# Attention preparation: head products copied to SBUF by ScalarE before the multiplications, column sums with the rows as moving operand, and the first transposes placed ahead of the weight preparation

## The chip, the cores and the metric

The kernel runs on one core of a Trainium2 chip. The metric is the device time of one execution in microseconds (us), taken as the median of several runs. Engines are named as in the profile: PE is TensorE, with PEld for its weight loads; DVE is VectorE; ACT is ScalarE; POOL is GpSimd; SP is SyncE, which here only issues DMAs.

## What is computed

The reference is a two-layer network over 4096 nodes with 256 features. Each layer is a graph attention followed by a feed-forward part, both with a residual. There are three attentions in all (one in layer 0, two in a row in layer 1), and the change touches the preparation of these three:

```python
def attention(x, adj, W, a1, a2):                 # 4 heads of 64
    h = einsum('nf,hfd->hnd', x, W)               # products
    f1, f2 = einsum('hnd,hd->hn', h, a1), einsum('hnd,hd->hn', h, a2)
    e = leaky_relu(f1[:, :, None] + f2[:, None, :], 0.2)
    e = where(adj > 0, e, -9e15)
    return elu(einsum('hnm,hmd->hnd', softmax(e), h))

x = x + attention(layernorm(x), adj, L0)          # g0
x = x + ffn30(layernorm(x))                       # 30 steps of tanh, silu, layernorm, matmul
x = x + attention(attention(layernorm(x), adj, L1a), adj, L1b)   # g1, g2
x = x + mixture_of_experts(layernorm(x))          # 6 experts, top 2
```

## The kernel before

All tiles have 128 partitions. The 4096 nodes are 32 tiles, worked in 8 groups (`NG`) of 4 tiles (`G`). One function, `attention`, is called three times, under the names g0, g1 and g2. It has two stages: a preparation, which this change edits, and a long main stage, which it leaves alone. The main stage cannot begin before the preparation's buffers are given back.

The preparation runs a loop over `g`. For each group it does the following.

- `load(g)` (L260) fetches the group's 512 rows, 512 KB, through SP's queue, two groups ahead. In g0 these land in the tile `t`, which has three buffers; in g1 and g2 in `rows`.
- `columns(g)` (L270) transposes the rows on PE (L114) and copies them out of PSUM on ACT as `xT` (L278, or L281 in g2, which collects the column sums `xs` as it copies). Where the input is normalised (`norm`, in g0 and g1), `over_std` computes 1/std: `bn_stats` and `bn_aggr` on DVE (L101, L103) and a power on POOL (L106).
- `products(g)` (L299) multiplies with the weights on PE (L307). Its results lie in two PSUM tiles, `ph0` and `ph1`, of two node tiles each, with 256 head products and 8 logit columns for each node tile. The pool has one buffer for each, so the next group's products can only be written when all readers of this group's are done. DVE takes the logits out as `fs` (L320 or L324) and forms `gm` (L328). ACT makes the exponentials `bd` (L331), POOL multiplies them with signs (L332) and with 1/std to `b` (L362). PE transposes the logits (L336) into a small PSUM tile `sp` with one buffer. In g0 and g1, PE also computes the sums of the rows weighted by 1/std (L344): the 128x128 blocks of rows are the weights loaded into the array, and 1/std is the moving operand, one column. ACT copies them to `xs` (L351) and the logits to `rt` (L353), which SP stores to `fd`.
- `upper(g)` (L367) multiplies the products, read from PSUM, with `b` into two tiles `v` (DVE, L377, four instructions of 128x512), and ACT writes their fp16 upper halves to `vals` (L384). POOL fills one column of each `v` (L373).
- `lower(g)` (L386) writes the fp16 lower halves on DVE (L389, two instructions of 128x1040).

In g0 the loop also turns the adjacency of the first four row tiles into masks: POOL issues the loads (L209), PE transposes (L219), DVE compares (L227, L229). After the loop the sums of `xs` are spread by POOL (L442) and multiplied with the weights on PE (L445), and ACT scales the result into `hs` (L446).

`weights(...)` gives for each attention a pair: `load`, whose DMAs ACT issues, and `make`, which computes the logit columns of the weights on DVE (L159, L160) and, with `norm`, subtracts their means (L166 on PE, L168 on DVE). The preparation of g0 carries out all three `make`: g0's own ahead of the loop, the others at `g` 3 and 5.

The order of the calls inside one round of the loop is: load(g+2), columns(g), products(g-1), lower(g-2), upper(g-1), masks. For the first two groups `columns(g)` comes after `lower(g-2)`. The order in which each engine's queue finally holds the instructions is set by the framework's planner from this program order and its own estimate of when each instruction can run. Only in the main stage is the order of DVE and ACT fixed by hand.

## Time and profile before

| | |
|---|---|
| median of 3 runs | 3557.42 us (3556.58 to 3568.16) |
| profiled execution, its own time | 3558.91 us |
| its span, first to last instruction | 3557.2 us |
| mean granted TensorE clock | 0.967 |
| preparation of g0, by the trace | from the start to 124.7 us |
| preparation of g1 | 1900 to 1988.9 us |
| preparation of g2 | 2566.5 to 2625.8 us |

The profiled execution lies 1.5 us above the median, so a difference worked out in its trace may be taken from either. The three preparations hold about 273 us of the span. The page's shares of busy time are means over stages with quite different limits, so the preparations are read by themselves: busy time by stretch, who waited for whom in a stretch, and the instructions in order of time. In the profile a matmul of two fp32 operands shows as two instructions, so `x16` on L307 is eight matmuls. In the view of instructions in order of time, a line gives start, duration, engine, line and operation, and in brackets the idle time of the engine before it with what ended it.

### The profile page before, as it was taken

The numbers are of one execution on the slowest core, as the hardware profiler recorded it, in microseconds if no ns is written. First come the engines' busy times: TensorE is split into PE (matmuls) and PEld (weight loads), VectorE is DVE, ScalarE is ACT, GpSimd is POOL, SyncE is SP. The second block draws the span as 40 slices with busy tenths as digits, with TensorE's granted clock in tenths as the row PEclk, the third lists the DMA queues.
The fourth block names the chain that finished last, engine by engine and source line by source line (L and its number), as shares of the span: only waits on it lengthen the run. The fifth ranks groups of instructions, "written<-read, shape, count | busy, mean of one in ns | idle before, by whom it ended". The sixth has DMA issues, their size and how long they took to land. (4 is left out here: it accounts for less than half of the span.)

```text
span 3557.2 us, 80784 instructions
## 1 busy us (share of the span) xinstructions
PE 3272.9 (92%) x33523; PEld 2963.8 (83%) x33523; DVE 3010.9 (85%) x6039; ACT 2613.4 (73%) x2902; POOL 1101.7 (31%) x899
## 2 busy tenths in 40 slices
PE   6889999996999999999998899999979999995995
PEld 5778888885888888888887799999869999993784
DVE  6899999997887877778787799999989999997445
ACT  2688888895766666666663799999879999992221
POOL 3210101004877777777772000000000000001662
PEclk8899999998999999999998899999999999997997
DMA  6796886602000000000006021313221331314224
GB/s 137 139 234 134 196 189 139 189 17 60 1 1 1 1 1 1 1 1 1 1 1 220 14 92 50 123 30 113 79 97 46 111 120 37 120 37 148 90 90 182
DMA packets 280200, 288.47 MB, mean 81 GB/s; under 512 B 97149, under 2 KB 230426, under 8 KB 279834
## 3 DMA queue, kind: packets, MB, share of 16 engines
q1 hardware_dynamic: 198770, 224.18, 19.2%
q0 software_dynamic: 73920, 52.97, 9.7%
q10 hardware_dynamic: 7144, 6.16, 0.6%
q8 instruction: 264, 4.33, 0.5%
q14 instruction: 102, 0.84, 0.1%
HBM read 248.01 MB, written 68.81 MB: 89 GB/s over the span
## 5 line engine op out<-in xcount | busy, mean ns | idle before, releaser
L556 PE MATMUL acc<-vals,m 128*128 128x130 f16 (+1 forms) x19456 | 1723.4, 233 | 83.0 <-DVE m L619 42.7
L470 ACT ACTIVATE st<-f1b,f2b 128x1024 bf16<-128x1024 f32 (+2 forms) x1664 | 1659.4, 1073 | 100.1 <-DVE m L604 92.1
L556 PEld LDWEIGHTS <-m 128*128 128x128 bf16 x19456 | 1518.3, 98 | 181.3 <-DVE m L619 64.9
L604 DVE TENSOR_TENSOR m<-st,m 128x2048 bf16<-128x2048 bf16 (+2 forms) x832 | 929.0, 1134 | 12.4 <-ACT st L470 12.3
L774 PE MATMUL po<-wT,zT 128*128 128x256 f32 x3840 | 874.1, 381 | 13.3 <-ACT zT L800 12.3
L774 PEld LDWEIGHTS po<-wT,zT 128*128 128x128 f32 x3840 | 713.6, 191 | 104.2 <-ACT zT L800 14.8
L556 PE MATMUL acc<-vals,rows 128*128 128x130 f16 x5120 | 614.1, 221 | 15.1 <-DVE rows L619 15.1
L760 POOL TENSOR_TENSOR th<-th,y 128x1024 f32<-128x1024 f32 x240 | 567.5, 2366 | 192.8 <-ACT th L759 192.2
L106 POOL TENSOR_TENSOR ln_rstd<-ln_rstd,mhalf 128x4 f32<-128x4 f32 x272 | 282.4, 1039 | 881.6 <-DVE ln_rstd L105 676.4
L556 PEld LDWEIGHTS <-rows 128*128 128x128 bf16 x5120 | 490.0, 96 | 20.5 <-DVE rows L619 20.1
L101 DVE BATCH_NORM_STATS2 ln_st<-z 128x6 f32<-128x256 f32 x960 | 338.0, 414 | 190.5 <-ACT z L765 190.5
L800 ACT COPY zT<-tp 128x1024 f32<-128x1024 f32 x240 | 242.7, 1011 | 323.8 <-PE tp L114 323.8
L619 DVE TENSOR_TENSOR rows<-m,m 128x2048 bf16<-128x2048 bf16 x320 | 391.7, 1224 | 10.2
L784 DVE SCALAR_TENSOR_TENSOR y<-po,ln_rstd,bias 128x256 f32<-128x256 f32 x928 | 378.8, 470 | 6.6 <-PE po L774 5.9
L765 ACT ACTIVATE z<-th 128x1024 f32<-128x1024 f32 x240 | 254.5, 1060 | 17.4 <-POOL th L760 17.4
L114 PE MATMUL tp<-ident,z 128*128 128x128 f32 x1920 | 250.8, 274 | 8.8 <-ACT z L765 7.9
L114 PEld LDWEIGHTS tp<-ident,z 128*128 128x128 f32 x1920 | 225.3, 141 | 35.5 <-ACT z L765 10.5
L759 ACT ACTIVATE th<-y 128x1024 f32<-128x1024 f32 x240 | 251.3, 1048 | 4.8 <-DVE y L784 4.7
L209 POOL DMA_DIRECT2D rows<-in_adj_dram x80 | 72.9, 912 | 497.3 <-PE tp_m L219 488.2
L619 DVE TENSOR_TENSOR m<-m,m 128x1792 bf16<-128x1792 bf16 (+1 forms) x200 | 202.2, 1011 | 13.0 <-PE acc L556 0.5
L449 POOL MEMSET hs<- 128x4 f32 x3 | 0.3, 102 | 607.2 <-DVE u L500 585.9
L307 PE MATMUL ph<-g_w,xT 128*128 128x264 f32 x384 | 120.0, 477 | 30.9 <-DVE v L377 27.4
(212 smaller groups left out, 2319.7 us busy)
## 6 DMA issues: line engine op xcount, KB each, us to landing
m<-edges SPq DMA_DIRECT2D x32, 2048.0 KB, 9.9
rows<-in_adj_dram POOLq DMA_DIRECT2D x64, 448.0 KB
edges<-ms SPq DMA_DIRECT2D x64, 448.0 KB, 5.0
m<-edges SPq DMA_DIRECT2D x16, 1792.0 KB
f1b<-fd SPq DMA_DIRECT2D x32, 512.0 KB, 3.4
rows<-x1d SPq DMA_DIRECT2D x16, 512.0 KB, 6.3
y<-yd SPq DMA_DIRECT2D x16, 512.0 KB, 9.5
f1b<-fd SPq DMA_DIRECT2D x16, 448.0 KB, 3.3
```

Source lines behind the costliest of these rows:

```text
L101: nc.vector.bn_stats(st[:, r, :], src[:, r, :])
L106: nc.gpsimd.tensor_tensor(rstd, rstd, mhalf, OP.pow)
L114: nc.tensor.transpose(ps[:, k, r * P : (r + 1) * P], src[:, r, k * P : (k + 1) * P], ident)
L470: nc.scalar.activation(steps[at][:, s, :w], f1b[c, h][:, :w], AF.Relu, bias=f2b[:, 2 * q + s, h : h + 1], scale=BIG)
L556: nc.tensor.matmul(acc[:, i, cols], lhs[:, s, rows], v[:, cols], start=(j == 0 and n_ == 0), stop=(j == NT - 1 and n_ == 1), skip_group_ch ...
L604: nc.vector.tensor_tensor(m1[:, :, :w], st[:, :, :w], m, OP.logical_and if turned(q) else OP.min)
L619: nc.vector.tensor_tensor(m2[:, :, :w], m, m1[:, :, :w], OP.subtract)
L759: nc.scalar.activation(th[at], y[:, g * G : (g + 1) * G, :], AF.Tanh, scale=0.01)
L760: nc.gpsimd.tensor_tensor(th[at], th[at], y[:, g * G : (g + 1) * G, :], OP.add)
L765: nc.scalar.activation(z, th.pop(at - 1), AF.Silu, scale=0.01)
L774: nc.tensor.matmul(po[:, r, :], src[:, k, r * P : (r + 1) * P], wT[:, k, :], start=(k == 0), stop=(k == KC - 1),)
L784: nc.vector.scalar_tensor_tensor(y[:, g * G + r, :], po[:, r, :], rstd[:, r : r + 1], last if end else bias, op0=OP.mult, op1=OP.add,)
```

## The change

It has four edits, all in the preparation.

1. `products(g)` has a new SBUF tile `hc` (128x1024, fp32, one buffer). ACT copies the head products of `ph0` and `ph1` into it, right after the logits of each are taken. `upper` reads `hc` in place of the PSUM tiles, with one 128x1024 multiplication for each `v` in place of two of 128x512.
2. With `norm`, the weighted sums of the rows are formed with 1/std (one column) as the loaded weights and the rows (256 columns) as moving operand: four matmuls a group into one partition of `sp`, in place of eight with a moving operand of one column. DVE copies or adds them into `xs`, now one row of 256; the copies on ACT go.
3. After the loop, with `norm`, two matmuls with one row each turn `xs` into a column, which DVE copies, in place of a reduction.
4. g0's own `make` runs after `columns(0)`, inside the first round of the loop, and no longer ahead of the loop. Its DMAs are issued where they were.

```diff
-                xs = prep.tile([P, KC, NG], F32, name="xs")
+                xs = prep.tile([1, C] if norm else [P, KC, NG], F32, name="xs")
...
+                    hc = work.tile([P, G, C], F32, name="hc", bufs=1)
                     for i, ph in enumerate(phs):
...
+                        nc.scalar.copy(hc[:, 2 * i : 2 * i + 2, :], ph[:, :, :C])
...
-                        for k in range(KC):
-                            for i in range(G):
-                                nc.tensor.matmul(
-                                    pt[:, P + k : P + k + 1],
-                                    n[:, i, k * P : (k + 1) * P],
-                                    stds[g][:, i : i + 1],
-                                    start=(i == 0),
-                                    stop=(i == G - 1),
-                                )
-                        nc.scalar.copy(xs[:, :, g], pt[:, P : P + KC])
+                        for i in range(G):
+                            nc.tensor.matmul(
+                                pt[:1, P : P + C],
+                                stds[g][:, i : i + 1],
+                                n[:, i, :],
+                                start=(i == 0),
+                                stop=(i == G - 1),
+                            )
+                        if g == 0:
+                            nc.vector.tensor_copy(xs, pt[:1, P : P + C])
+                        else:
+                            nc.vector.tensor_tensor(xs, xs, pt[:1, P : P + C], OP.add)
...
-                    for i, ph in enumerate(phs):
-                        for part in range(2):
-                            nc.vector.tensor_tensor(
-                                vs[part][:, 2 * i : 2 * i + 2, :, :D],
-                                ph[:, :, :C].rearrange("p i (h o) -> p i h o", h=H),
-                                b[:, part, 2 * i : 2 * i + 2, :, None].to_broadcast([P, 2, H, D]),
-                                OP.mult,
-                            )
+                    for part in range(2):
+                        nc.vector.tensor_tensor(
+                            vs[part][:, :, :, :D],
+                            hc.rearrange("p i (h o) -> p i h o", h=H),
+                            b[:, part, :, :, None].to_broadcast([P, G, H, D]),
+                            OP.mult,
+                        )
...
-                if late:
-                    late.pop(0)()
...
                     if g < 2:
                         columns(g)
+                    if g == 0 and late:
+                        late.pop(0)()
...
-                nc.vector.tensor_reduce(xt, xs, axis=AX.X, op=OP.add)
+                if norm:
+                    pt = small_ps()
+                    for k in range(KC):
+                        nc.tensor.matmul(
+                            pt[:, k : k + 1], xs[:, k * P : (k + 1) * P], ones[:1, :1], start=True, stop=True
+                        )
+                    nc.vector.tensor_copy(xt, pt[:, :KC])
+                else:
+                    nc.vector.tensor_reduce(xt, xs, axis=AX.X, op=OP.add)
```

## The prediction, made before the change was run

> **What bounds the kernel now.** Of the three preparations I first read the busy time by stretch. One row each for g0, g1 and g2: start:end, length, then busy us of PE, PEld, DVE, ACT and POOL, the granted clock, the DMA share and GB/s.

> ```profile
> 22.00:124.70 102.70, 78.50 (x454) 64.84 (x454) 67.49 (x166) 29.70 (x57) 31.20 (x62) 0.79 0.63 122
> 1900.00:1987.40 87.40, 70.41 (x336) 57.15 (x335) 59.27 (x155) 32.27 (x59) 17.36 (x50) 0.80 0.48 165
> 2566.50:2625.80 59.30, 42.63 (x207) 33.91 (x207) 47.26 (x85) 32.43 (x75) 7.56 (x34) 0.96 0.60 206
> ```

> No engine is full: PE and DVE are busy 66 to 81% of the time, ACT 29 to 55%. So the groups are bound by waits on one another. Next, one group of g1 in order of time:

> ```profile
> 1962.92 2.48 DVE L377 TENSOR_TENSOR v<-ph,b 128x512 f32<-128x512 f32 x4 [1.45 <-POOL b L362]
> ...
> 1964.35 5.49 PE L307 MATMUL ph<-g_w,xT 128*128 128x264 f32 x16 [1.00 <-DVE v L377]
> ...
> 1969.88 0.17 DVE L320 TENSOR_TENSOR fs<-ph,ln_rstd 128x16 f32<-128x16 f32 x1 [1.21 <-PE ph L307]
> ...
> 1970.35 0.51 ACT L331 ACTIVATE bd<-gm,lnscale 128x16 f32<-128x16 f32 x2 [3.39 <-DVE gm L328]
> ...
> 1971.23 0.24 POOL L362 TENSOR_TENSOR b<-bd,ln_rstd 128x32 f32<-128x32 f32 x1
> ```

> This is a ring. PE may write `ph0` only when DVE has read it for both `v` (1.43 us after 1962.92). It takes 5.5 us, then come logits, exponentials and `b`, and at 1971.51 the next `v`: 8.6 us a round. I take the period from first to last `v`: g0 34.06 to 119.18 in 7 steps, 12.16 us; g1 1913.75 to 1982.33, 9.80; g2 2574.82 to 2620.32, 6.50. In g2 the ring is hidden by another chain (the chain of waits; start, us):

> ```profile
> 2607.71 1.90 DVE v L377 x3
> 2609.64 0.04 issue
> 2609.69 1.10 ACT vals L384
> 2610.81 1.24 DVE vals L389
> ```

> DVE does three of four multiplications before ACT can write `vals`, and then waits for it. The table of waits in g0 shows which waits belong to the ring and which don't:

> ```profile
> ACT xs L351 <- PE sp L344: 36.6, 8, 6.8
> ...
> ACT vals L384 <- DVE v L377: 20.7, 8, 3.4
> ...
> PE ph L307 <- DVE v L377: 10.2, 6, 2.5
> ```

> ACT's 36.6 us are the longest and cost least: it has spare time there.

> [...] the 16 product instructions take 3.8 us at best and 5.5 to 6.8 us in many groups of g0 and g1 (clock 0.79 and 0.80), mostly 3.8 in g2 (0.96). [...] the power on POOL takes 1.02 us as median, and 1.89 where it starts under L389, which has two SBUF inputs:

> ```profile
> 63.25 1.24 DVE L389 SCALAR_TENSOR_TENSOR vals<-vals,v 128x1040 f16<-128x1040 f16 x1
> ...
> 63.50 1.89 POOL L106 TENSOR_TENSOR ln_rstd<-ln_rstd,mhalf 128x4 f32<-128x4 f32 x1 [3.29 <-DVE ln_rstd L105]
> ```

> [...]

> **The change part by part, a group.**

> Removed on DVE: four L377, 2.48 us from first start to last end. Added: two of 1024 elements; L389, nearly as wide and also from SBUF, does two in 2.40, so 2.3 us: -0.18. In g0 and g1 DVE also gets the add into `xs`, 256 elements on one partition: 0.42 (L159, SBUF) to 0.47 (L784, PSUM), about 0.4 in a row: net +0.22.

> Added on ACT: two copies of 128x512 out of PSUM. L281 takes 0.588 and L479 0.595 for such a size, so 1.1 us; the copy L351 (0.16) goes. ACT a group in g2: `xT` 1.15, `vals` 2.06, `bd` 0.4, `rt` 0.2, copies 1.1, in sum 4.9.

> PE: the sums now are 8 instructions in place of 16. The old ones start 0.115 us apart (1.84 in all). The new ones stream 256 columns; L307 with 264 starts every 0.213: 1.7 us, or 3.4 at half clock. So this alone saves 0.1 us, or costs 1.6.

> What matters is the ring. `ph` is now free after the logits and a copy, and PE's products of the next group run under the exponentials, `v` and `lower` of this one, which are the cover. `vals` of part 0 can be written while DVE does part 1. What is late next is bounded from two sides.

> Lower bound, DVE packed without gaps. DVE's busy time in 34 to 119 is 55.46 of 85 us, so 7.93 a period; g1 48.35 in 70 us from 1915, 6.77; g2 35.73 in 44 us from 2576, 5.28. With the changes above: 8.15, 7.0, 5.1.

> Upper bound, the new ring run serially. `hc` has one buffer, so ACT's copies for group g wait for `v` of g-1, and behind them in ACT's queue stand the exponentials. Ring: `v` 2.35, second `vals` 1.1, `xT` 1.0, copies 1.1, exponentials 0.5, then POOL's three instructions up to `b`, each blocked by one DVE instruction, 3 x 1.15: 9.5 in g1. g0 adds POOL's issue of an adjacency load (L209, 0.83) and one more blocking: 11.5. In g2 `b` is `bd`: `v` to exponentials 6.2 with its `xT` of 1.15, and 0.35 where the sign (L332) is blocked: 6.55.

> I take the middle, since ACT can put `xT` under `v`, but the queues hold their order. g0 9.83, g1 8.25, g2 5.83; times seven steps -16.3, -10.9 and -4.7, in sum -31.9 us.

> The end of g0 and g1: the way to `hs` gets two small matmuls and a copy (0.3, 0.2, and 0.2 of waits), the add for the copy and reduction (+0.1): +0.6 if nothing blocks. POOL's spread L442 now may stand under one or two `v`, up to +2.9. Before, ACT did `hs` ahead of the last `vals` in g1 (1.6 us of DVE's idle time), so it is partly on the path. I take 1.5 each: +3.0.

> The moved `make`: on DVE four products (0.42), two reductions (0.67), two subtractions (0.42), on PE four instructions; no DMA. I cost it at nothing. The transposes on PE come earlier (only one ran, at 5.36, and the other seven at 17.2, behind L166's wait for weights), but their reader can't:

> ```profile
> 18.66 0.83 ACTq L151 DMA_DIRECT2D g_ab<-in_L_gnn_a_dram  x1
> ...
> 19.53 1.28 ACT L278 ACT_TABLE_LOAD   x1 [19.53 <-DMA g_ab<-in_L_gnn_a_dram]
> ```

> ACT is in its DMA issues until 19.5, then loads its table, copies `xT` to 21.83, and the products start at 21.88. The weights are ready at 19.1, so `make` may come 2.7 us later for nothing; beyond that it costs what it exceeds. A gain needs ACT free earlier: none to 3 us; I take 0.

> Sum: -31.9 + 3.0 = -28.9. The profiled execution of 3558.91 gives 3530.0; the median, 1.5 lower, gives **3528.5 us**.

> **The rivals.**

> *DVE packed.* Planner and queues fit, the clock stays up: 7 x (4.01 + 2.80 + 1.40) = 57.5, less 3.0: 3503. For it: ACT has room in g0 and g1. Against: DVE was never over 81% in these stages.

> *The serial ring.* [...] 7 x (0.66 + 0.30 - 0.05) = 6.4, less 3.0: 3554, no change. For it: both POOL and ACT stand in `b`'s way, and in g2 ACT is at 4.9 of 5.8 us.

> *DVE waits for the sums.* Before, ACT waited for L344, 36.6 us in g0, under cover. Now DVE, the busiest engine here, waits, with `lower` and `v` queued behind, and ACT and PE waiting for those. After the logits PE needs 0.27 for L336 and 1.7 for the sums, 3.7 in all at half clock, and more if products of the next group stand ahead. A wait of w in 16 groups cancels the gain at w = 1.8 us and makes the kernel slower by 0.3% at 2.5. At 3 us: 48 - 28.9 = +19, 3576.5. Against it: PE is freer, the clock should hold, and `lower` can be placed ahead of the add.

> *It doesn't do what it says.* If the planner leaves the products behind `v`, as it now puts group 7's transposes (83.88) ahead of group 5's products, the ring stays; that ends in the serial ring's time.

> **How the numbers follow.** A measurement of this kernel can tell about 0.3%, 10.7 us, from no change. The forecast has a chance of 0.54 (3512 to 3546, faster), DVE packed 0.12 (faster), the serial ring 0.17 (0.16 within, 0.01 faster), DVE waiting for sums 0.17 (0.15 slower, 0.02 within). So faster 0.67, same 0.18, slower 0.15. The range of 3507 to 3560 leaves out half of the packed case and most of the slow one.

> **What would show it.** Right: `v` every 9 to 10.5 us in g0, 7.5 to 9 in g1, 5.5 to 6.2 in g2; L307's waits name the copies on ACT in place of L377, its 16 instructions mostly take 3.8 us, the clock in g0 and g1 is above 0.9; the first product stays at 21.9. Wrong: the DVE add waits over 1.8 us a group for PE, POOL's `b` chain takes 3 us or more with DVE idle, the products still start after `v`, or time changes in the main stages.

## The result, and the profile after

The changed kernel takes 3522.96 us (median of four runs, 3520.33 to 3527.76), the kernel before, run beside it, 3562.79 (3556.58 to 3568.26): ratio 0.989, 95% interval 0.9865 to 0.9916. The forecast was 3528.5 in a range of 3507 to 3560, with 0.67 for faster. So sign and range held. But the forecast counted 28.9 us of gain; the medians differ by 39.8 us (34.5 from 3557.42, the median that the forecast started from), and in the traces the three preparations gained 45.5. The experiments below show where the difference came from.

First the same three stretches as before, busy time by stretch: start:end, length, busy us of PE, PEld, DVE, ACT, POOL with instruction counts, then granted clock, DMA share, GB/s.

```profile
22.00:101.30 79.30, 66.15 (x387) 45.45 (x388) 67.76 (x159) 38.51 (x65) 33.52 (x61) 0.98 0.69 134
1877.00:1948.50 71.50, 59.01 (x278) 38.77 (x277) 60.42 (x147) 40.71 (x67) 24.79 (x50) 0.95 0.58 201
2528.50:2583.40 54.90, 41.86 (x199) 32.81 (x199) 44.30 (x68) 39.69 (x92) 30.38 (x34) 0.94 0.65 217
```

DVE has nearly the busy time that it had (67.76 us in g0, 67.49 before), in 79 us in place of 103. PE has less (66.15 for 78.50, 59.01 for 70.41), although it now streams 256 columns for each sum. The clock was 0.79 and 0.80 in g0 and g1 and is 0.98 and 0.95.

Next one group of g1, instructions in order of time:

```profile
1919.72 2.36 DVE L382 TENSOR_TENSOR v<-hc,b 128x1024 f32<-128x1024 f32 x2 [0.26 <-POOL b L368]
...
1919.84 3.73 PE L308 MATMUL ph<-g_w,xT 128*128 128x264 f32 x16
...
1923.82 1.07 ACT L328 COPY hc<-ph 128x512 f32<-128x512 f32 x2 [0.56 <-DVE fs L322]
1923.87 1.23 DVE L394 SCALAR_TENSOR_TENSOR vals<-vals,v 128x1040 f16<-128x1040 f16 x1
...
1924.22 1.89 PE L347 MATMUL sp<-rows,ln_rstd 128*1 128x256 f32 x8
...
1925.22 0.51 ACT L335 ACTIVATE bd<-gm,lnscale 128x16 f32<-128x16 f32 x2 [0.33 <-DVE gm L332]
...
1926.43 3.73 PE L308 MATMUL ph<-g_w,xT 128*128 128x264 f32 x16
...
1927.25 2.36 DVE L382 TENSOR_TENSOR v<-hc,b 128x1024 f32<-128x1024 f32 x2 [0.59 <-POOL b L368]
```

The products run beside `v` and no longer after it: 1919.84 beside 1919.72, 1926.43 ahead of 1927.25. They take 3.73 us both times (5.49 in the group shown of before). The copies of `hc` wait for the logits (L322), which DVE reads from the same PSUM tile. From first to last `v` the period is 8.84 us in g0 (33.69 to 95.57 in 7 steps; 12.16 before), 7.14 in g1 (9.80) and 5.85 in g2 (6.50).

The tables of DVE's waits, first in g0 and then in g1 (us in total, times, longest):

```profile
DVE xs L357 <- PE sp L347: 0.8, 1, 0.8
...
DVE xs L355 <- PE sp L347: 3.6, 1, 3.6
DVE v L382 <- POOL b L368: 3.0, 5, 1.0
```

In all 16 groups DVE waits twice for the sums, 4.4 us, of which 3.6 in the first group of g1. The rival that feared this wait is out.

### The profile page after: what moved, and what is told of

Same layout as the page of the kernel before. It is cut to its first block, busy times and chain, and to the rows that moved or that the text cites. A ratio compares the mean times of both kernels' runs of the same rounds, so it can differ in the third digit from the quotient of the medians.

```text
span 3522.9 us, 80529 instructions
## 1 busy us (share of the span) xinstructions
PE 3251.1 (92%) x33403; PEld 2927.4 (83%) x33403; DVE 3009.0 (85%) x6007; ACT 2638.3 (75%) x2934; POOL 1136.6 (32%) x899
## 4 chain that ended last, share of the span: by engine, by line
PE 40%; DVE 33%; issue 14%; POOL 5%; ACT 5%; DMA 2%; another core or an unknown queue 0%; ACTq 0%; DVEq 0%; POOLq 0%; SPq 0%
PE po L787 22%; DVE m L617 17%; PE acc L569 9%; PE tp L114 6%; ACT st L483 3%; DVE rows L632 3%; DVE m L632 2%; POOL yd L1193 2%; POOL gx L1127 2%; DVE v L382 1%; DVE u L496 1%; DVE ms L229 1%; DVE u L506 1%; DVE u L510 1%; DVE u L518 1%
## 5 line engine op out<-in xcount | busy, mean ns | idle before, releaser
L483 ACT ACTIVATE st<-f1b,f2b 128x1024 bf16<-128x1024 f32 (+2 forms) x1664 | 1659.1, 1073 | 98.2 <-DVE m L617 91.7
L106 POOL TENSOR_TENSOR ln_rstd<-ln_rstd,mhalf 128x4 f32<-128x4 f32 x272 | 286.8, 1055 | 872.1 <-DVE ln_rstd L105 652.6
L632 DVE TENSOR_TENSOR rows<-m,m 128x2048 bf16<-128x2048 bf16 x320 | 391.7, 1224 | 10.2
L114 PEld LDWEIGHTS tp<-ident,z 128*128 128x128 f32 x1920 | 224.9, 141 | 35.9 <-ACT z L778 10.7
L209 POOL DMA_DIRECT2D rows<-in_adj_dram x80 | 72.9, 912 | 490.9 <-PE tp_m L219 478.3
L1155 ACT COPY w<-ew 128x512 f32 x37 | 22.7, 618 | 129.1 <-PE ph L1162 66.5
```

Of the source, the lines that this page charges most:

```text
L106: nc.gpsimd.tensor_tensor(rstd, rstd, mhalf, OP.pow)
L114: nc.tensor.transpose(ps[:, k, r * P : (r + 1) * P], src[:, r, k * P : (k + 1) * P], ident)
L483: nc.scalar.activation(steps[at][:, s, :w], f1b[c, h][:, :w], AF.Relu, bias=f2b[:, 2 * q + s, h : h + 1], scale=BIG)
L632: nc.vector.tensor_tensor(m2[:, :, :w], m, m1[:, :, :w], OP.subtract)
```

## The experiments

**Which edit does it?** The kernel before, the kernel after and three kernels with a part of the change each, all on one chip. The columns give, from each trace: first step L483 (L470 before) of g0's main stage; first `v` to first step of g1 and of g2; clock from first to last `v` in g0 and g1.

| kernel | median us | ratio to before (interval) | g0 ends | g1 | g2 | clock g0, g1 |
|---|---|---|---|---|---|---|
| before | 3564.61 | | 124.7 | 75.1 | 51.0 | 0.79, 0.79 |
| after, again | 3519.66 | 0.9883 (0.9863 to 0.9902) | 102.6 | 58.3 | 46.2 | 0.97, 1.00 |
| sums only | 3528.93 | 0.9902 (0.9886 to 0.9917) | 100.8 | 62.2 | 51.5 | 1.00, 1.00 |
| `hc` only | 3540.68 | 0.9934 (0.9920 to 0.9949) | 114.5 | 61.8 | 46.2 | 0.84, 0.89 |
| `make` moved only | 3569.72 | 1.0014 (1.0008 to 1.0021) | 126.5 | 74.9 | 51.0 | 0.80, 0.79 |

The kernel after, unchanged:

> The changed kernel again, as the measure for the parts run beside it. Both theories: 0.989 of before (0.987 to 0.992), periods of v 8.8 us in g0, 7.1 in g1, 5.9 in g2. If the 8.2 us by which the expert loop at the end was longer in the first trace of the changed kernel belong to the change, they are there again (gathers from first to the last stage's first add 243 us, before 235); if they are variation of that loop, this trace can show anything from 235 to 244.

Measured 3519.66, 45.0 us below the kernel before on the same chip. The g0 end of 102.6 is the measure of how far one trace repeats another (101.3 in the first). The part after g2, with the loop over the experts, took 939.5 us in the first trace and 935.0 in this one, so its length there doesn't belong to the change.

The kernel before with edits 2 and 3 alone:

```diff
-   nc.tensor.matmul(pt[:, P + k : P + k + 1], n[:, i, k * P : (k + 1) * P], stds[g][:, i : i + 1], ...)
+   nc.tensor.matmul(pt[:1, P : P + C], stds[g][:, i : i + 1], n[:, i, :], ...)
```

> Only edits 2 and 3 (sums with the rows moving), products still read from PSUM. Ring theory (the gain is PE's freedom from v): the ring stays, PE still idles in it, so at most the clock's share is won: periods above 11 us in g0 and 9 in g1, g2 unchanged at 6.5, time 3 to 12 us below before. Clock theory (the gain is an array kept at full clock by 256 moving columns in place of one): the clock in g0 and g1 goes from 0.80 to above 0.93, the 16 product instructions take 3.8 us, and the time falls by 20 us or more.

Edit 1 alone:

```diff
+   nc.scalar.copy(hc[:, 2 * i : 2 * i + 2, :], ph[:, :, :C])
...
-   ph[:, :, :C].rearrange("p i (h o) -> p i h o", h=H),
+   hc.rearrange("p i (h o) -> p i h o", h=H),
```

> Only edit 1 (products copied to SBUF, multiplied from there), sums by the old matmuls. Ring theory: 28 to 38 us below before, periods below 9.5 us in g0, 8 in g1, 5.9 in g2, and the clock rises by itself [...]. Clock theory: the clock stays near 0.80 in g0 and g1, and the time falls by 20 us at most, 5 of them in g2.

Edit 4 alone:

```diff
-                if late:
-                    late.pop(0)()
...
+                    if g == 0 and late:
+                        late.pop(0)()
```

> Only edit 4 (g0's weight preparation after its first transposes). Prediction's view: nothing, within 2 us of before; the first product starts at 21.9 us (between 21.5 and 22.7) because ACT copies xT only after its DMA issues. Rival: the earlier transposes let products start 2 us or more earlier, and the first v with them.

The sums alone bring 35.7 us and `hc` alone 23.9, together 59.6, while the whole change brings 45.0 (and 45.0 without edit 4, below): they repair partly the same thing. The sums alone do what the clock theory said: clock 1.00, and more than 20 us. `hc` alone lies between its two theories: it raises the clock only to 0.84 and 0.89, and brings less than the 28 us of the one and more than the 20 of the other. The sums, which the prediction priced at "save 0.1 us, or cost 1.6" a group, end g0 as early as the whole change does, with the products still read from PSUM. In g2, which has no such sums, only `hc` acts (46.2 with it, 51.5 without). Edit 4 by itself costs 5.1 us by the medians, which neither of its expectations allowed: the first product starts at 21.92, as the first said, but 1.8 us more stand at g0's end, and the rest is in no stage that I could name.

**Why do the sums matter: the clock, or ScalarE's queue?** In the kernel before, ACT's queue in g0 had the copy that waits for the sums ahead of the exponentials; so the sums could have held up the ring. Or the one-column matmuls left the clock low. Two kernels on one chip (before there: 3566.03) were to tell. The first moves only the copy:

```diff
-   nc.scalar.copy(xs[:, :, g], pt[:, P : P + KC])
+   nc.vector.tensor_copy(xs[:, :, g], pt[:, P : P + KC])
```

> The kernel before, with only the copy of the old column sums into xs moved from ScalarE to VectorE; matmuls and buffers as before. In the kernel before, ScalarE's queue in g0 has the copies that wait for the sums ahead of the exponentials; here the exponentials stand first. In g1 of the kernel before they stood first for most groups already. Queue theory (the sums held the exponentials back, and so the ring): g0's first step starts at 105 to 113 us in place of 124.7, g1 unchanged within 2 us (75.1 from first v to first step), g2 51.0; time 10 to 20 us below before. Clock theory (the one-column matmuls leave TensorE at 0.79, which is what costs): clock stays at 0.79 to 0.82, g0's first step at 120 to 126, time within 4 us of before.

The second adds the new sums to the old ones and lets nobody read them:

```diff
+   for i in range(G):
+       nc.tensor.matmul(pt[:1, P + KC : P + KC + C], stds[g][:, i : i + 1], n[:, i, :], ...)
    for k in range(KC):
        for i in range(G):
            nc.tensor.matmul(pt[:, P + k : P + k + 1], n[:, i, k * P : (k + 1) * P], stds[g][:, i : i + 1], ...)
```

> The kernel before, with the sums of moving rows added beside the old column sums; nobody reads the added ones, ScalarE copies the old ones as before. More work on TensorE: 64 instructions in g0 and 64 in g1, 1.7 us a group at full clock. Clock theory: the granted clock rises to over 0.95 in g0 and g1, and g1 gets shorter in spite of the work: 62 to 67 us from first v to first step (75.1 before), its products mostly 3.8 us; g0's first step at 102 to 110 us (the planner here also puts the exponentials first, as in the run with the copy on VectorE), time 15 to 30 us below before. If instead the gain came from the shorter way of the sums to their reader or from the fewer instructions: clock 0.79 to 0.85, g1 75 to 85 us, time equal to before or up to 15 us above.

With the copy on DVE: 3566.3, ratio 1.0002 (0.9994 to 1.0011), clock 0.80 and 0.76. The time is level, but the stages are not: g0 ends at 120.4, 4.3 us earlier, and g1 takes 79.4, 4.3 us longer. DVE now waits for the old sums, 9.8 us in 8 waits in g0 and 13.9 in 8 in g1. So the clock theory has the time and g0's end right, but ACT's queue was worth something in g0. The kernel before shows how, in order of time:

```profile
42.17 0.17 DVE L328 TENSOR_TENSOR gm<-fs,mb 128x16 f32<-128x16 f32 x1
...
44.39 0.16 ACT L351 COPY xs<-sp 128x2 f32<-128x2 f32 x1 [6.28 <-PE sp L344]
...
44.60 0.50 ACT L331 ACTIVATE bd<-gm,lnscale 128x16 f32<-128x16 f32 x2
```

The exponentials (L331) could start when `gm` is there, at 42.34, and start at 44.60, behind the copy that waits for the sums. It is so in all 8 groups of g0, 1.2 to 2.5 us each, 15.8 in sum; with the copy on DVE the same distance is at most 0.11 us. From its first `v` to its first step g0 then takes 85.1 us in place of 90.6, in spite of DVE's waits.

With both sums: 3538.51, ratio 0.9921 (0.9907 to 0.9934), clock 1.00 in both, g0's end at 105.0, g1 66.6. More work on PE makes the kernel 27.5 us faster, and all of these numbers lie in what the clock theory gave. For g1 this answers the question: its exponentials stood ahead of the copy in 6 of 8 groups before, so the 8.5 us that g1 gains, with more work on PE, are mainly the clock's. For g0 it doesn't: there the exponentials now stand first too, so its 72.9 us in place of 90.6 hold both the clock and the order of ACT's queue, and no run here parts them. Behind the exponentials ACT's wait for the old sums (19.9 us in g0, 20.6 in g1) is cheap: the kernel with the new sums alone gains only about 8 us more on before (35.7 against 27.5, each beside its own runs of before), and it also has less work on PE.

The same 30 us of g1 by stretch, in the kernel before, with both sums, with the sums edit alone, and in the kernel after:

```profile
1915.00:1945.00 30.00, 26.37 (x126) 21.63 (x126) 21.03 (x61) 11.95 (x20) 5.64 (x15) 0.79 0.65 228
```

```profile
1915.00:1945.00 30.00, 28.80 (x161) 21.52 (x160) 23.36 (x62) 13.05 (x24) 7.42 (x20) 1.00 0.43 151
```

```profile
1915.00:1945.00 30.00, 23.31 (x108) 15.84 (x108) 24.90 (x61) 12.61 (x20) 6.54 (x19) 1.00 0.24 85
```

```profile
1915.00:1945.00 30.00, 23.33 (x111) 14.80 (x110) 27.43 (x60) 19.70 (x33) 11.03 (x24) 1.00 0.31 108
```

PE's busy share does not tell the clock: 26.37 of 30 us at 0.79, but 23.31 at 1.00, since a slow matmul is also busy longer (the 16 product instructions take 5.49 us in place of 3.73).

What does? In the kernel before, stretches of half clock (granted 0.50, and 1.00 between them) begin in g1 at 1914.09, 1927.74, 1937.98, 1948.22, 1965.29, 1972.12 and 1982.36 us, whole multiples of 3.41 us apart, and all but the last, which runs on past the loop, last 3.41 or 6.83 us. So I divided the trace from 1907.26 to 1982.36 into pieces of this length. It has 14 pieces of 3.41 us at full clock, and 7 of them are followed by half clock; PE is busy for 1.61 to 3.06 us in them, and for 2.63 to 3.41 in the 7 that are followed by full clock, so its busy time doesn't part the two. Without the one-column matmuls it does: 0.36 to 1.60 us before half clock, 1.74 to 3.12 before full. In the kernel with the copy on DVE the same count gives 0 to 1.42 and 1.71 to 3.42; with `hc` alone it is at most 1.22 before half clock and at least 1.57 before full. Two pieces in which PE has nothing but sums, each with the piece that follows; first one-column sums, in the kernel with the copy on DVE, then 256-column sums, in the kernel with the sums edit alone (its next half clock begins at 1951.57, nine steps after 1920.85):

```profile
1907.73:1911.14 3.41, 1.75 (x17) 1.66 (x15) 1.21 (x3) 1.96 (x4) 0.82 (x4) 1.00 1.11 370
1911.14:1914.56 3.42, 3.04 (x10) 2.55 (x11) 2.81 (x5) 2.06 (x2) 0.00 (x0) 0.50 1.02 330
```

```profile
1920.85:1924.26 3.41, 1.83 (x9) 0.53 (x8) 2.54 (x11) 1.42 (x4) 0.83 (x4) 1.00 0.26 104
1924.26:1927.67 3.41, 3.25 (x15) 2.82 (x16) 3.13 (x8) 2.06 (x2) 1.04 (x1) 1.00 0.04 10
```

PE is busy for 1.75 us in the one and 1.83 in the other, and the products that follow run at a granted clock of 0.50 in the one and of 1.00 in the other. In these traces, then, a piece of 3.41 us with 3.06 us of busy time, 1.82 of it one-column matmuls, was followed by half clock (the piece before 1972.12 us). What in such a piece sets the clock of the next was not measured apart from this.

**What the moved `make` costs beside the other edits.** The kernel after without edit 4 (the call stands ahead of the loop again), and on the same chip the kernel after with the sign and `b` on DVE:

> The kernel after without the moved make (make stands ahead of the loop again). Theory that the move costs at the start (VectorE's work on the other stages' weights stands between the first products and their readers): first v at 29.5 to 31 us in place of 33.7 to 34.6, all later steps earlier by the same, time 2 to 5 us below after (3515 to 3521). Theory that the move is worth nothing either way (the gain at the start is given back because g0 is bound later by loads or by TensorE's transposes): first v earlier, g0's first step still at 100.8 to 102.6, time 3518 to 3525. Theory that the move brings something: time 3525 or more.

Measured 3521.01, ratio 0.9873 (0.9858 to 0.9888), which can't be told from after. The trace shows the cost and where it goes: first `v` at 30.8 (33.7 with the move), g0's end at 100.1 (101.3). So 2.9 us at the start shrink to 1.2 by the end of g0 (3.8 and 2.5 against the second trace of the kernel after), which lies between the first two theories. In the kernel after, DVE at the start of g0, in order of time:

```profile
21.02 0.43 DVE L159 TENSOR_TENSOR prod<-g_w,g_ab 128x256 f32<-128x256 f32 x1 [0.92 <-DMA g_ab<-in_L_gnn_a_dram]
21.37 0.76 DVE L168 TENSOR_TENSOR g_w<-g_w,sp 128x264 f32<-128x264 f32 x2
```

g0's own weights (L168) now stand behind a product (L159) that waits for a transfer; L168 ran at 18.39 before. The products start at 22.58 in place of 21.89, and the planner puts four transposes of the adjacency between them; they take 6.25 us from first to last in place of 3.83, which is the larger part of the delay.

**GpSimd in the way.** The next suspicion came from g2 of the kernel after, in the chain of waits (start, us, what):

```profile
2555.39 0.21 ACT bd L335
...
2555.66 1.27 POOL v L379
2556.93 0.17 POOL bd L336
...
2557.12 1.23 DVE v L382
```

POOL's fill of one column of `v`, 128x16, takes 0.21 us in the three of g2's 16 fills that start ahead of L382, and 1.21 to 1.27 in the 13 that start beside it, as long as L382 itself. L382 has two SBUF inputs now; L377 had one, and in g2 of the kernel before all 16 fills, which ran beside it, took 0.21. Test: POOL's sign and `b` go to DVE, in the kernel after.

```diff
-   nc.gpsimd.tensor_tensor(bd[:, 1], bd[:, 1], sign[:, at, None].to_broadcast([P, G, H]), OP.mult)
+   nc.vector.tensor_tensor(bd[:, 1], bd[:, 1], sign[:, at, None].to_broadcast([P, G, H]), OP.mult)
...
-   nc.gpsimd.tensor_tensor(b, bd, stds.pop(g)[:, None, :, None].to_broadcast([P, 2, G, H]), OP.mult)
+   nc.vector.tensor_tensor(b, bd, stds.pop(g)[:, None, :, None].to_broadcast([P, 2, G, H]), OP.mult)
```

> The kernel after with the sign of the exponentials and the product with ln_rstd (b) on VectorE in place of GpSimd. Theory that GpSimd, blocked by VectorE's two-input instructions (1.27 us in place of 0.2), stands on g2's path: first v to first step in g2 43 to 44.5 us in place of 46.2 and in g1 55 to 57 in place of 57.9, time 3 to 7 us below after. Theory that VectorE is the bound there and GpSimd only fills its gaps: VectorE gets 0.1 to 0.2 us more a group in g2 and 0.3 in g0 and g1, g2 46 to 47.5, time equal to after or up to 5 us above.

Measured 3517.0, ratio 0.9865 (0.9850 to 0.9880). g1 is 55.6 (57.9), g2 44.7 (46.2), g0's end 100.0 (101.3), 5.1 us in sum (the 1.3 of g0 is no more than two traces of the kernel after differ by): the POOL theory, though g2 gained 0.2 less than it gave. In this piece of its chain of waits in g2 POOL is gone, and DVE does the sign in 0.09 us:

```profile
2556.16 1.23 DVE v L382
2557.39 0.09 DVE bd L336
...
2557.56 1.18 DVE v L382
```

**Two further waits of the new kernel.** ACT's copies of a PSUM tile wait for DVE's logits. In the kernel after, the copies take the 8 logit columns along, and DVE reads them from `hc`:

```diff
-   f = ph[:, :, C : C + 2 * H]
+   nc.scalar.copy(hc[:, 2 * i : 2 * i + 2, :], ph[:, :, : C + 2 * H])
+   f = hc[:, 2 * i : 2 * i + 2, C : C + 2 * H]
```

> The kernel after, with ScalarE's copies taking the logits' 8 columns a tile along and VectorE reading the logits from hc in SBUF. In the kernel after, ScalarE's copies of a bank wait for VectorE's read of the logits from that bank. Theory that this wait holds up the products (TensorE gets ph back later by it): products start earlier after hc's copies, first v to first step in g1 54 to 57 us (57.9) and in g2 43.5 to 45.5 (46.2), time 4 to 10 us below after. Theory that the order only shifts the wait (VectorE's logits then wait for ScalarE's copy, behind hc's one buffer, which waits for the last v): logits later by 0.6 to 1.1 us a group, g1 58 to 64 us, g2 46 to 50, time equal to after or up to 15 us above.

Measured 3532.98, ratio 0.9909 (0.9892 to 0.9926), g1 61.6 and g2 49.1: the second theory. The waits in 2540 to 2575 us of the kernel after, and then of this one:

```profile
PEld ph L308 <- ACT hc L328: 3.6, 5, 1.5
```

```profile
PEld ph L308 <- ACT hc L319: 7.4, 5, 1.7
```

The logits came out of PSUM at once; now they stand behind a copy that needs `hc` free, and the products wait longer, not less. In its chain of waits in g2 two of POOL's fills, of 1.27 us each, stand in each round ahead of the copies, so they have a part in the loss. The wait of the copies for the logits was the cheaper one.

The end of g1: in the chain of waits of the kernel after, POOL's spread and four slow matmul instructions (2.09 us; 1.12 in g2) stand between the last `lower` and the first step.

```profile
1943.59 1.15 DVE vals L394
1944.74 0.08 DVE xt L451
...
1944.87 1.45 POOL xsb L455
...
1946.36 2.09 PE sp L458 x4
```

In the kernel after, the spread by two matmuls and one copy on ACT:

```diff
-   nc.tensor.matmul(pt[:, k : k + 1], xs[:, k * P : (k + 1) * P], ones[:1, :1], start=True, stop=True)
-   nc.vector.tensor_copy(xt, pt[:, :KC])
-   nc.gpsimd.tensor_copy(xsb, xt[:, :, None].to_broadcast([P, KC, P]))
+   nc.tensor.matmul(pt[:, k * P : (k + 1) * P], xs[:, k * P : (k + 1) * P], ones[:1, :], start=True, stop=True)
+   nc.scalar.copy(xsb, pt[:, : KC * P].rearrange("p (k n) -> p k n", k=KC))
```

> The kernel after, with the sums spread over the partitions by two matmuls against a row of ones and one copy on ScalarE, in place of two small matmuls, a copy on VectorE and the spread on GpSimd (L455, 1.44 us at the end of g1). Theory that the way to hs stands on the path at the end of g1: lower there ends at 1946.05 and the first step starts at 1948.76; with the spread off GpSimd the first step follows lower by 1.0 to 1.6 us, v to first step 55.8 to 57.0 (57.9), time 1 to 3 us below after (g0 gives under 0.5). Theory that something else holds the first step (its masks, f1's rows): g1 57.6 to 58.3, no change in time beyond 1 us.

g1 is 56.6 (57.9), the time 3521.65 (0.9883, 0.9863 to 0.9904): the first theory by the trace, and too small for the measured time to tell. The copy now stands behind a `vals` of 1.09 us on ACT, and L458 still takes 2.09.

**A better version.** Without the move, with the sign and `b` on DVE and this spread:

> The kernel after without the moved make, with the sign and b on VectorE and the sums spread by matmuls: three pieces, of which two were measured alone on this chip (first step of g0 1.2 us earlier without the move; 1.3 to 1.7 us of g0, 2.3 to 2.7 of g1 and 1.5 of g2 with the products on VectorE). If they add up, with 1 to 2 us for the spread: first steps 7 to 10 us earlier than in the kernel after in sum, time 3511 to 3516. If the spread's gain is the same as that of the products on VectorE (both relieve GpSimd at the end of g1): time 3515 to 3519.

> The run with the three pieces, and the logits taken along into hc as in the first run of this batch. If the copies' wait for the logits' read matters more once the other waits are gone: 2 to 6 us below the run with the three pieces. If the logits come later by ScalarE's copy: equal to it or up to 12 us above.

The first takes 3514.35 us, ratio 0.9856 (0.9835 to 0.9877): g0's end at 97.6, g1 55.1, g2 45.0, in sum 7.7 us of the preparations less than after (3.7, 2.8 and 1.2), as expected if the pieces add up. It has the lowest time of all kernels here, though its interval and that of after overlap. With the logits taken along it is 3524.0 (0.9884, 0.9864 to 0.9905), the loss of the single test again. A second buffer for `hc`, which might loosen the wait of the copies for `v`, wasn't tried.

## Why the prediction was right in sign and short in size

Term by term, from the profiled executions:

| term | predicted us | measured us |
|---|---|---|
| g0, 7 periods | -16.3 (to 9.83) | -23.2 (to 8.84) |
| g1, 7 periods | -10.9 (to 8.25) | -18.6 (to 7.14) |
| g2, 7 periods | -4.7 (to 5.83) | -4.6 (to 5.85) |
| ends of g0 and g1 | +3.0 | +0.2 and +1.3 |
| moved `make`, first `v` | 0 | -0.4, of which the move +2.9 |

With 0.2 less at the end of g2 the preparations gained 45.5. The two profiled spans differ by only 34.3 (3557.2 and 3522.9). Of the missing 11.2, 8.1 lie after g2's first step, where the kernel before has 931.4 us and after 939.5. That part of the kernel isn't touched, and the other traces have 935.0 to 939.2 there, those with the copy on DVE and with `make` moved among them (938.4 and 936.4). So the profiled execution of before was short there; the pair measured again gave 45.0 between medians. The other 3.1 us lie between the stages, 0.6 ahead of g1's first `v` and 2.5 ahead of g2's; the second trace of the kernel after has 585.6 us ahead of g2 where before has 585.9, so they too can be variation.

That the forecast came so near is partly luck. It gave 31.9 us to the ring that `hc` breaks, and `hc` alone brings 23.9; it gave next to nothing to the sums, and they bring 35.7 alone; and the two overlap.

**The step that failed is the price of the sums edit.** "So this alone saves 0.1 us, or costs 1.6" counted the time of the instructions, and nearly right: they take 1.89 us a group, and 3.45 in the one group of after, the first of g1, that fell into a granted clock of 0.50. Their effect on everything behind them was 35.7 us. The prediction had the clock and the slow products in hand ("5.5 to 6.8 us in many groups of g0 and g1 (clock 0.79 and 0.80)") and expected `hc` to mend both ("PE is freer, the clock should hold"), an assumption of the author that no trace of before had shown. But `hc` alone left the clock at 0.84 and 0.89. g2, with the same ring, the same `ph` and a clock of 0.96, pointed the right way: it has no such sums. The upper and lower bounds were built from the ring and from DVE's busy time; with the clock up, g1 came to 7.14, close to the packed bound of 7.0, and DVE is busy 27.43 of 30 us there. g0 with 8.84 stays above its 8.15.

**ACT's 36.6 us of waiting "are the longest and cost least":** wrong for g0. ACT had spare time, but the exponentials stood behind the waiting copy and started 1.2 to 2.5 us late in each group, and they are part of the ring. The prediction read the ring in a group of g1, where they stood first, and priced the copy that goes (L351) at its 0.16 us. In g1, and behind the exponentials, the wait is cheap: the run with both sums has 40 us of it.

**g2's 5.83 was hit (5.85)**, and the mechanism named for it was there: the products under `v`, then POOL blocked for one DVE instruction on the way to it. The 0.35 us counted for this block in the upper bound, the author's estimate, is 1.27 in the chain; that the middle of the bounds was taken hid the miss, so the exact hit is luck.

**The ends:** +3.0 was twice what came. Small matmuls, copy and a slow spread on POOL are on g1's path (1.3 us), on g0's hardly (0.2).

**The moved `make` at nothing:** wrong by 2.9 us at the start and 1.2 at g0's end. The argument looked at ACT, which is busy with its DMA issues, and at how late the weights might come. It missed DVE's queue, where L168 came behind other weights' L159, and the products themselves, which took 6.25 us with transposes among them. "The first product stays at 21.9" became 22.58.

**The signs to look for:** the clock above 0.9 and products of 3.8 us came true, though not by the edit that was to bring them. Waits of L308 that name ACT's copies came in g2. `v` every 9 to 10.5 and 7.5 to 9 us was passed on the good side. The slower rival, DVE waiting for the sums, needed 1.8 us a group; it had 4.4 in sixteen groups.

## What to carry to other kernels

Ask of small matmuls not only what they take, but what they leave TensorE's clock at: here the stages whose equal matmuls took 3.8 us at one time and 5.5 to 6.8 at another had a clock to win (0.79 and 0.80, now 0.98 and 0.95), and the sibling stage that kept it (0.96) told which instructions to suspect. Swapping the roles, so that one column is loaded and the wide operand moves, takes nearly the same time here (1.89 us a group, 1.84 before) and was worth more than the buffer that broke the ring (35.7 us alone, against 23.9). Don't write off an engine's long wait because it has spare time: ask what stands behind it in the queue, and in every stage, not in one. A copy out of PSUM then pays by what it frees, but a two-input VectorE instruction whose source moved from PSUM to SBUF held up GpSimd's copies here (1.27 us in place of 0.21), so look at what GpSimd has on the path.
